# A graph attention layer's main loop: one-hot columns made a step ahead, two chunks of edges a PSUM bank, later copies and lasting count tiles

## The chip, the cores and the metric

The kernel runs on one core of one Trainium2 chip. The metric is the device time of one execution in microseconds (us); the times given are medians of several runs. The core has five engines with queues of their own: TensorE (PE; its weight loads appear as PEld), VectorE (DVE), ScalarE (ACT), GpSimd (POOL) and SyncE (SP), which here only issues transfers. Each queue is worked off in order.

## The reference

Two rounds of (graph layer, expert layer) over 3125 nodes with 256 features and 100000 edges sorted by destination. The change lies wholly in the first graph layer's first attention convolution:

```python
def gat_conv(x, src, dst, W, a_src, a_dst, bias, concat):
    N = x.shape[0]
    H, C = a_src.shape
    h = (x @ W).reshape(N, H, C)
    al_s = jnp.einsum('nhc,hc->nh', h, a_src)
    al_d = jnp.einsum('nhc,hc->nh', h, a_dst)
    e = jax.nn.leaky_relu(al_s[src] + al_d[dst], NEG_SLOPE)
    m = jax.ops.segment_max(e, dst, num_segments=N)
    ex = jnp.exp(e - m[dst])
    denom = jax.ops.segment_sum(ex, dst, num_segments=N)
    alpha = ex / denom[dst]
    out = jax.ops.segment_sum(h[src] * alpha[:, :, None], dst, num_segments=N)
    out = out.reshape(N, H * C) if concat else out.mean(axis=1)
    return out + bias
...
    loop = jnp.arange(N, dtype=edge_index.dtype)
    src = jnp.concatenate([edge_index[0], loop])
    dst = jnp.concatenate([edge_index[1], loop])
    h = gat_conv(x, src, dst, W1, att_src1, att_dst1, b1, concat=True)
    h = graph_norm(h, gn_w, gn_b, gn_ms)
    h = jax.nn.relu(h)
    out = gat_conv(h, src, dst, W2, att_src2, att_dst2, b2, concat=False)
```

There are four heads in the first convolution (W1 is 256 x 1024). Everything after it (graph norm, the second convolution, the expert layers, two graph convolutions) is untouched.

## The kernel before

Class `FirstLayer` does two jobs in one loop (`run`, from L2147 on), because both go through the edges in the same order of destinations.

**Counts.** The later layers want a matrix of edge counts, source by destination. The edges are taken in 391 chunks of 256 (`C1`, two columns of 128 each, `CT`). For a chunk, `make` builds two one-hot tiles for each column, `hot_key` (DVE, L1696) and `hot_lo` (DVE in L1699 for the first 20 chunks and every third one, else ACT in two steps, L1702 and, in `sharpen`, L1709). `multiply` (L1711, matmul in L1716) takes their product into a PSUM bank `ps` of three. `keep` (L1727) copies its columns but the first into the tile `acc` (ACT, L1733), and `add` (L1738) adds the first column (DVE, L1741), since neighbouring chunks share it. In pass i of the loop `count_step` (L1772) makes chunk i, multiplies i−1, keeps i−2 and adds i−3. The destinations are cut into ten pieces of 320 (`GS`, `GC`); at a piece's first chunk (`CUT`) `piece` (L1677) takes an `acc` tile of a pool of two, clears a part of it (L1686) and copies the 100 columns that the last piece has run over into it (L1688); `add_own` and `store_counts` then finish the last piece and write it to DRAM. `low_degrees` sums the first piece over PE (L1766).

**Edge sums.** For destinations from 256 on (`DN`), 283 chunks (`NE`), the layer is done sparsely. `fetch` (L1832) has POOL gather the 256 source rows of a chunk from a table in DRAM, two indirect transfers of 128 rows (L1834), into a ring `edge_rows` of 12 chunks (`RB`·`BC`); the place of a chunk is free when the chunk 12 earlier has been multiplied. Four chunks are a batch. One batch ahead of their use, `pick_terms` (PE, L1872, into a bank `aux` of two), `sum_terms` (DVE, L1881, which reads the bank and the gathered rows of the whole batch), `pick_slope` (L1888), `weigh_edges` (ACT, L1893) and `spread_edges` (DVE, L1899) make the weights. `multiply_edges` (L1903, eight matmuls in L1913) sums a chunk into one of four half banks `ps_edge`, and `add_edges` (L1918, DVE, L1926) adds this to `agg1`, a tile of 384 destinations (`GA`), one chunk later. `edge_step` (L1929) orders these. A finished tile of `agg1` goes through W1: `through_w1` (L2002) loads the inverse sums, scales on DVE (L2034) and has eight products (PE, L2042, into an `aux` bank); `put_first` (L2050) copies each from PSUM (ACT, L2053), stores it (L2054) and leaves its `bn_stats` (DVE, L2056) to the next pass. These are tasks in a queue, one a pass.

**Dense part.** The 256 first destinations are done with the counts of piece 0: `slope` and `exponent` on ACT, `weigh` on DVE, `multiply_dense` on PE (L2102), then `dense_end` and `dense_first`, which use `aux` banks too.

The order on PE, DVE and ACT within the loop is the order of the code (`in_order`, L108). The queues of SP and POOL are ordered by the scheduling of the whole program. So POOL also holds, from 693 us on, loads of x for a later stage between the gathers (L989). Where instructions use a position known only at run time, `where` (L1527) loads eight positions into registers at a time (`RG`). Passes before the loop (from L2194) do the first chunks; the loop runs until both jobs and all tasks are through. `d0` is the pass at which the dense part may begin, `share` the number of edge steps due.

Of the kernel before, what the change touches and what calls it, by code (L numbers as in the profile page):

```python
# [24 lines left out]
P = 128  # L25
# [23 lines left out]
RG = 8  # L49
# [1344 lines left out]
class FirstLayer:  # L1394
# [261 lines left out]
    def open_counts(self, ctx, pool):  # L1656
# [14 lines left out]
        self.acc_pool = ctx.enter_context(tc.tile_pool(name="acc", bufs=2, reuse_waits="tile"))  # L1671
        self.hot = ctx.enter_context(tc.tile_pool(name="hot", bufs=3, reuse_waits="tile"))
# [4 lines left out]
    def piece(self, g):  # L1677

        nc = self.nc
        acc = self.acc[g] = self.acc_pool.tile([P, NB, GC + EXT], F16, name="acc")
        if g == 0:
            nc.vector.memset(acc, 0.0)
        else:
            nc.vector.memset(acc[:, :, EXT if g in (1, GS - 1) else GC:], 0.0)  # L1686
        if g:
            nc.vector.tensor_copy(acc[:, :, :EXT], self.acc[g - 1][:, :, GC:])  # L1688
# [73 lines left out]
    def low_degrees(self):  # L1762
        nc = self.nc
        pd = self.aux.tile([P, 512], F32, name="aux")[:, :DN]
        for j in range(NB):
            nc.tensor.matmul(pd, lhsT=self.ones, rhs=self.acc[0][:, j, :DN], start=(j == 0),  # L1766
                             stop=(j == NB - 1))
        sums = self.work.tile([1, DN], F32, name="deg_low")
        nc.scalar.copy(sums, pd[0:1, :])
        nc.sync.dma_start(self.deg_row.rearrange("b p -> (b p)")[None, :DN], sums)  # L1770

    def count_step(self, i, beside=(lambda: None,) * 2):  # L1772
# [3 lines left out]
        if 1 <= i <= C1:  # L1776
            self.multiply(i - 1)
        if 3 <= i <= C1 + 2:
            self.add(i - 3)
        if 2 <= i <= C1 + 1:  # L1780
            self.keep(i - 2)
# [3 lines left out]
        if i == C1 + 2:  # L1785
            self.tasks.append(lambda: self.add_own(GS - 1))
            self.tasks.append(lambda: self.store_counts(GS - 1))
# [3 lines left out]
    def open_sums(self, ctx, w1, stats):  # L1791
# [11 lines left out]
        self.ps_edge = [banks[i % 2][:, i // 2 * 256:(i // 2 + 1) * 256] for i in range(4)]  # L1803
# [23 lines left out]
        self.ready, self.scaled, self.later = 0, 0, []  # L1827
# [101 lines left out]
    def edge_step(self, c):  # L1929
# [18 lines left out]
        if 0 < c <= NE:  # L1948
            self.add_edges(c - 1)
# [52 lines left out]
    def through_w1(self, q):  # L2002
# [34 lines left out]
        def product(h, f):  # L2037
            bank = (self.ps_counts.tile([P, 512], F32, name="ps") if self.counted else
                    self.aux.tile([P, 512], F32, name="aux"))
# [9 lines left out]

    def put_first(self, h, f, n0, n, ph, piece, true):  # L2050
        nc = self.nc
        out = self.work.tile([P, GA], F32, name="first", bufs=3)[:, :n]
        nc.scalar.copy(out, ph)  # L2053
        nc.sync.dma_start(self.first[h, :, f, n0:n0 + n], out)  # L2054

        self.later.append(lambda: nc.vector.bn_stats(self.stats[:, h, f, piece, :],  # L2056
                                                     out[:, :true]))
# [7 lines left out]
    def lead(self, s):  # L2065
# [5 lines left out]
        if j == 0:  # L2071
            pt = self.aux.tile([P, 512], F32, name="aux")
# [39 lines left out]
    def dense_end(self, i, po, turned):  # L2112
        nc = self.nc
        inv = self.work.tile([P, 1], F32, name="inv", bufs=4)
# [5 lines left out]
        def turn():  # L2120
            pt = self.aux.tile([P, 512], F32, name="aux")
# [6 lines left out]
    def dense_first(self, h, f, turned):  # L2128
        ph = self.aux.tile([P, 512], F32, name="aux")[:, :DN]
# [17 lines left out]
    def run(self, src_cols, dst_cols, dst_rows, x_in, keep, stats, u2):  # L2147

        tc, nc, k, I = self.tc, self.nc, self.k, self.I
        with ExitStack() as ctx:  # L2150
# [82 lines left out]
            i0, d0 = i, CUT[1] + 6  # L2233
# [5 lines left out]
            while i < C1 + 3 or e <= NE or s < last_s or self.tasks or self.later:  # L2239
# [9 lines left out]
                if i < C1 + 3:  # L2249
# [4 lines left out]
                self.counted = i >= C1 + 3  # L2254
                if i == d0:
                    self.lead(0)
                later, self.later = self.later, []
                if self.tasks:
                    self.tasks.popleft()()
                share = (FIRST * (i - i0) / (d1 - i0) if i < d1 else  # L2260
                         FIRST + (NE + 1 - FIRST) * (i - d1) / (C1 - d1))
                while e <= NE and e <= share:
                    self.edge_step(e)
                    if e == NE:
# [6 lines left out]
                if due:  # L2271
                    self.dense_step(s)
                    s += 1
                for f in later:
# [536 lines left out]
```

## Time and profile before

| | us |
|---|---|
| median of 7 runs (lowest to highest) | 2381.84 (2375.16 to 2385.69) |
| the profiled execution, its own time | 2379.65 |
| span of its profile | 2377.9 |
| before the first gather of rows | 0 to 84.9 |
| the loop, to the last W1 product | 84.9 to 899.8 |
| the later layers | to 2377.9 |
| busy over the span: PE, DVE, ACT, POOL | 2058.2, 1328.8, 1088.4, 808.9 |

Over the 820 us from 85 to 905, PE was busy 659.2 us, DVE 621.4, ACT 500.6 and POOL 603.3. The groups that the loop spends most on, with their busy time and mean length: gathers on POOL, L1834, 566 of 1.04 us (588.5); edge matmuls, L1913, 2264 of 0.29 us (331.0); one-hot columns on DVE, L1696, 782 of 0.33 us (234.8); count matmuls, L1716, 782 of 0.34 us (193.1); copies of counts on ACT, L1733, 391 of 0.46 us (178.3). A busy share says how long an engine worked, not whether anything else waited for it; for that the waits and the timeline are read.

In a row of a timeline the first number is the start, the second the length, both in us; what stands in brackets is how long the engine was idle before, and the instruction that ended this. A row of a wait lists the engine and line that waited, what it waited for, the total, the number of times and the longest.

### The profile page before, as it was taken

The numbers are of one execution on the slowest core, as the hardware profiler recorded it, in microseconds if no ns is written. First come the engines' busy times: TensorE is split into PE (matmuls) and PEld (weight loads), VectorE is DVE, ScalarE is ACT, GpSimd is POOL, SyncE is SP. The second block draws the span as 40 slices with busy tenths as digits, with TensorE's granted clock in tenths as the row PEclk, the third lists the DMA queues.
The fourth block names the chain that finished last, engine by engine and source line by source line (L and its number), as shares of the span: only waits on it lengthen the run. The fifth ranks groups of instructions, "written<-read, shape, count | busy, mean of one in ns | idle before, by whom it ended". The sixth has DMA issues, their size and how long they took to land. (4 is left out here: it accounts for less than half of the span.)

```text
span 2377.9 us, 35928 instructions
## 1 busy us (share of the span) xinstructions
PE 2058.2 (87%) x10508; PEld 1714.5 (72%) x10508; DVE 1328.8 (56%) x4374; ACT 1088.4 (46%) x2506; POOL 808.9 (34%) x802
## 2 busy tenths in 40 slices
PE   5377887878888878899998799979988979999996
PEld 5255766666676656788887688858877767888885
DVE  6988676777888672178888243333326664221221
ACT  4297656556666446044444244434434433222221
POOL 1477777777777732000001300000001213222221
PEclk9999999999999889999999799989999988999998
DMA  8445475756767759962221100033334435667772
GB/s 263 114 122 157 131 211 141 208 166 187 203 183 227 202 163 344 316 218 70 70 70 46 36 1 1 1 124 111 111 112 155 149 134 181 188 195 229 206 224 59
DMA packets 236987, 358.49 MB, mean 151 GB/s; under 512 B 37357, under 2 KB 178052, under 8 KB 233068
## 3 DMA queue, kind: packets, MB, share of 16 engines
q1 hardware_dynamic: 193611, 256.27, 33.5%
q0 software_dynamic: 39600, 95.33, 15.8%
q10 hardware_dynamic: 3568, 4.47, 0.7%
q8 instruction: 88, 1.44, 0.3%
q14 instruction: 120, 0.98, 0.1%
HBM read 270.26 MB, written 86.20 MB: 150 GB/s over the span
## 5 line engine op out<-in xcount | busy, mean ns | idle before, releaser
L1834 POOL DMA_INDIRECT edge_rows<-table,pick x566 | 588.5, 1040 | 177.8 <-issue 84.6
L1913 PE MATMUL edge_sums<-edge_moves,edge_rows 128*128 128x120 f32 x2264 | 331.0, 293 | 76.9 <-DVE agg L1926 74.0
L1913 PEld LDWEIGHTS edge_sums<-edge_moves,edge_rows 128*128 128x128 f32 x2264 | 308.3, 206 | 114.0 <-DVE agg L1926 90.6
L1092 PE MATMUL po<-parts,cnt_r 128*128 128x512 f32 x1250 | 318.5, 410 | 17.7 <-ACT cnt_r L1086 9.5
L1092 PEld LDWEIGHTS po<-parts,cnt_r 128*128 128x128 f32 x1250 | 240.1, 195 | 71.6 <-ACT cnt_r L1086 10.3
L854 PE MATMUL po<-h,w 128*128 128x257 f32 x1250 | 278.9, 384 | 7.2 <-DVE w L845 4.9
L854 PEld LDWEIGHTS po<-h,w 128*128 128x128 f32 x1250 | 237.4, 191 | 44.3 <-DVE w L845 6.9
L1716 PE MATMUL ps<-hot_key,hot_lo 128*128 128x350 f16 (+2 forms) x782 | 193.1, 336 | 83.9 <-DVE acc L1741 38.4
L1733 ACT CAST acc<-ps 128x325 f32 (+2 forms) x391 | 178.3, 456 | 143.5 <-PE ps L1716 107.5
L1696 DVE TENSOR_SCALAR hot_key<-iota_key,key 128x350 f16<-128x350 f16 (+2 forms) x782 | 234.8, 329 | 3.4 <-PE ps L1716 1.9
L2679 ACT ACTIVATE hid<-ph,ffn_b 128x256 f32<-128x256 f32 (+1 forms) x232 | 105.6, 455 | 264.3 <-PE ph L2677 261.8
L2677 PE MATMUL ph<-xe,ffn_w 128*128 128x256 f32 (+1 forms) x928 | 194.8, 368 | 3.8 <-DVE rt_xt L1023 3.8
L2692 POOL DMA_INDIRECT out<-y,to x53 | 82.6, 1558 | 316.8 <-DVE y L2691 172.6
L2687 PE MATMUL py<-ffn_w,hid 128*128 128x256 f32 x848 | 189.8, 381 | 0.4 <-ACT hid L2679 0.4
L2677 PEld LDWEIGHTS ph<-xe,ffn_w 128*128 128x128 f32 x928 | 165.3, 194 | 27.2 <-DVE rt_xt L1023 4.2
L2687 PEld LDWEIGHTS py<-ffn_w,hid 128*128 128x128 f32 x848 | 159.3, 191 | 21.1 <-ACT hid L2679 0.8
L839 ACT ACTIVATE z<-z,att_cols 128x640 f32<-128x640 f32 x125 | 103.1, 828 | 154.1 <-DVE z L837 131.3
L1702 ACT ACTIVATE hot_lo<-iota_key,lo 128x128 f16<-128x128 f16 x494 | 169.6, 394 | 0.0
L1716 PEld LDWEIGHTS <-hot_lo 128*128 128x128 f16 x782 | 73.2, 104 | 129.0 <-ACT hot_lo L1709 41.2
L1086 ACT CAST cnt_r<-cnt_h 128x1920 fp32r<-128x1920 f16 x50 | 89.8, 1799 | 117.1 <-PE po L1092 106.6
L2353 POOL IOTA earlier<- 128x128 f32 x1 | 0.2, 243 | 399.9 <-PE po L1092 399.9
L845 DVE TENSOR_TENSOR w<-z,cnt 128x640 f32<-128x640 f32 x125 | 106.7, 854 | 38.6 <-PE po L854 35.6
(419 smaller groups left out, 3245.4 us busy)
## 6 DMA issues: line engine op xcount, KB each, us to landing
ffn_w<-in_L_ffn_W SPq DMA_DIRECT2D x58, 1024.0 KB
cnt_h<-cnt SPq DMA_DIRECT2D x50, 800.0 KB
rows<-blank SPq DMA_DIRECT2D x109, 258.0 KB
cnt<-acc SPq DMA_DIRECT2D x50, 400.0 KB
cnt<-cnt SPq DMA_DIRECT2D x25, 800.0 KB
normed<-first_out SPq DMA_DIRECT2D x20, 640.0 KB
first_out<-first SPq DMA_DIRECT2D x56, 192.0 KB
edge_rows<-table,pick POOLq DMA_INDIRECT x566
```

Source lines behind the costliest of these rows:

```text
L845: nc.vector.tensor_tensor(w, zs.pop(t), cnts[u, g, j // 5][:, j % 5, :], ALU.mult)
L854: nc.tensor.matmul(pos[i][:, :D + 1], lhsT=w[:, ts(i, P)], rhs=moving[:, j, :D + 1], start=(j == 0), stop=(j == NB - 1))
L1092: nc.tensor.matmul(pos[b], lhsT=c[:, j - j0, ts(b, P)], rhs=parts[i][:, j].rearrange("p a m -> p (a m)"), start=(j == 0), stop=(j == NB - 1))
L1696: nc.vector.tensor_scalar(h[:, u, :NB * w], self.wide[:, :NB * w], self.key[:, t:t + 1], None, op0=ALU.is_equal)
L1702: nc.scalar.activation(l[:, u, :], self.wide[:, :P], AF.Abs, bias=self.lo[:, t:t + 1], scale=-1.0)
L1716: self.nc.tensor.matmul(ps[:, :n], lhsT=l[:, u, :], rhs=h[:, u, :n], start=(u == 0), stop=(u == CT - 1))
L1733: ins = self.nc.scalar.copy(self.acc[g][:, :, ds(o + 1, width(c) - 1)], self.parts[c][:, :, 1:])
L1834: self.nc.gpsimd.indirect_dma_start(out=self.ring[:, e % (RB * BT), :], out_offset=None, in_=self.table, in_offset=bass.IndirectOffsetOnAx ...
L1913: nc.tensor.matmul(ps[:, f * 4 * w:f * 4 * w + EW], lhsT=self.rows_of(m)[:, e, ts(f, P)], rhs=self.spread[m % 3][:, e * 5 * w:e * 5 * w + EW],
L2677: nc.tensor.matmul(ph, lhsT=w1[:, c, ts(f, P)], rhs=xe[:, c, :], start=(c == 0), stop=(c == 1))
L2679: nc.scalar.activation(hid[:, f, :], ph, AF.Gelu, bias=b1[:, f:f + 1])
L2687: nc.tensor.matmul(py, lhsT=hid[:, f, ts(i, P)], rhs=w2[:, f, :], start=(f == 0), stop=(f == NF - 1))
```

## The change

It alters the order of the loop and what lies in which bank; what is computed stays.

- `RG` goes from 8 to 16: positions are loaded sixteen at a time.
- `acc` is no longer a pool of two tiles taken anew for each piece, but two lasting tiles used in turn. The part beyond column 100 is cleared for pieces 1 and 9 alone; for pieces 2 to 8 the clearing of the last 100 columns is left out.
- The one-hot tiles have four buffers instead of three, and `count_step` multiplies chunk i−2, adds i−4 and keeps i−3. The loop is a pass longer, and `d0` a pass later.
- `ps_edge` holds chunks 0 and 1 of four in one bank and 2 and 3 in the other, where it held 0 and 2, and 1 and 3. `add_edges` comes two chunks after the product.
- `put_first` only notes its copy; the copy and the store are issued at the end of the next pass, and `bn_stats` a pass after that. A new `bank` hands out the `aux` banks: it keeps the copy that is still owed for the bank given out two requests earlier, and issues it first. `pick_terms` goes on taking its `aux` bank without it.
- `inv` has two buffers instead of four.

```diff
-RG = 8
+RG = 16
...
-        self.acc_pool = ctx.enter_context(tc.tile_pool(name="acc", bufs=2, reuse_waits="tile"))
-        self.hot = ctx.enter_context(tc.tile_pool(name="hot", bufs=3, reuse_waits="tile"))
+        room = ctx.enter_context(tc.tile_pool(name="acc", bufs=1, reuse_waits="tile"))
+        self.both = [room.tile([P, NB, GC + EXT], F16, name=f"acc{i}") for i in range(2)]
+        self.hot = ctx.enter_context(tc.tile_pool(name="hot", bufs=4, reuse_waits="tile"))
...
-        acc = self.acc[g] = self.acc_pool.tile([P, NB, GC + EXT], F16, name="acc")
+        acc = self.acc[g] = self.both[g % 2]
         if g == 0:
             nc.vector.memset(acc, 0.0)
-        else:
-            nc.vector.memset(acc[:, :, EXT if g in (1, GS - 1) else GC:], 0.0)
+        elif g in (1, GS - 1):
+            nc.vector.memset(acc[:, :, EXT:], 0.0)
         if g:
             nc.vector.tensor_copy(acc[:, :, :EXT], self.acc[g - 1][:, :, GC:])
...
-        if 1 <= i <= C1:
-            self.multiply(i - 1)
+        if 2 <= i <= C1 + 1:
+            self.multiply(i - 2)
+        if 4 <= i <= C1 + 3:
+            self.add(i - 4)
         if 3 <= i <= C1 + 2:
-            self.add(i - 3)
-        if 2 <= i <= C1 + 1:
-            self.keep(i - 2)
+            self.keep(i - 3)
...
-        self.ps_edge = [banks[i % 2][:, i // 2 * 256:(i // 2 + 1) * 256] for i in range(4)]
+        self.ps_edge = [banks[i // 2][:, i % 2 * 256:(i % 2 + 1) * 256] for i in range(4)]
...
-        if 0 < c <= NE:
-            self.add_edges(c - 1)
+        if 2 <= c <= NE + 1:
+            self.add_edges(c - 2)
...
+    def bank(self):
+
+        first = self.held.popleft()
+        self.held.append(None)
+        if first in self.copies:
+            self.copies.remove(first)
+            first()
+        return self.aux.tile([P, 512], F32, name="aux")
+
     def put_first(self, h, f, n0, n, ph, piece, true):
         nc = self.nc
         out = self.work.tile([P, GA], F32, name="first", bufs=3)[:, :n]
-        nc.scalar.copy(out, ph)
-        nc.sync.dma_start(self.first[h, :, f, n0:n0 + n], out)
-
-        self.later.append(lambda: nc.vector.bn_stats(self.stats[:, h, f, piece, :],
-                                                     out[:, :true]))
+
+        def copy():
+            nc.scalar.copy(out, ph)
+            nc.sync.dma_start(self.first[h, :, f, n0:n0 + n], out)
+            self.later.append(lambda: nc.vector.bn_stats(self.stats[:, h, f, piece, :],
+                                                         out[:, :true]))
+        if not self.counted:
+            self.held[-1] = copy
+        self.copies.append(copy)
...
-            i0, d0 = i, CUT[1] + 6
+            i0, d0 = i, CUT[1] + 7
...
-            while i < C1 + 3 or e <= NE or s < last_s or self.tasks or self.later:
+            while i < C1 + 4 or e <= NE + 1 or s < last_s or self.tasks or self.later or \
+                    self.copies:
...
                 later, self.later = self.later, []
+                copies = list(self.copies)
                 if self.tasks:
                     self.tasks.popleft()()
                 share = (FIRST * (i - i0) / (d1 - i0) if i < d1 else
-                         FIRST + (NE + 1 - FIRST) * (i - d1) / (C1 - d1))
-                while e <= NE and e <= share:
+                         FIRST + (NE + 2 - FIRST) * (i - d1) / (C1 - d1))
+                while e <= NE + 1 and e <= share:
...
+                for f in copies:
+                    if f in self.copies:
+                        self.copies.remove(f)
+                        f()
                 for f in later:
                     f()
```

In `low_degrees`, `lead`, `dense_end`, `dense_first` and the products of `through_w1`, `self.aux.tile(...)` becomes `self.bank()`.

More of the change, by code (lines that the diff above doesn't have):

```diff
@@ L1763, in low_degrees @@
         nc = self.nc
-        pd = self.aux.tile([P, 512], F32, name="aux")[:, :DN]
+        pd = self.bank()[:, :DN]
         for j in range(NB):
@@ L1784, in count_step @@
         beside[1]()
-        if i == C1 + 2:
+        if i == C1 + 3:
             self.tasks.append(lambda: self.add_own(GS - 1))
@@ L1826, in open_sums @@
         self.agg = {}
-        self.ready, self.scaled, self.later = 0, 0, []
+        self.ready, self.scaled, self.later, self.copies = 0, 0, [], []
+        self.held = deque([None, None])
     def rows_of(self, m):
@@ L2038, in product @@
             bank = (self.ps_counts.tile([P, 512], F32, name="ps") if self.counted else
-                    self.aux.tile([P, 512], F32, name="aux"))
+                    self.bank())
             ph = bank[:, :n]
@@ L2071, in lead @@
         if j == 0:
-            pt = self.aux.tile([P, 512], F32, name="aux")
+            pt = self.bank()
             for i in range(DB):
@@ L2113, in dense_end @@
         nc = self.nc
-        inv = self.work.tile([P, 1], F32, name="inv", bufs=4)
+        inv = self.work.tile([P, 1], F32, name="inv", bufs=2)
         nc.vector.tensor_scalar(inv, po[:, ONE:], 1e-30, None, op0=ALU.max)
@@ L2120, in turn @@
         def turn():
-            pt = self.aux.tile([P, 512], F32, name="aux")
+            pt = self.bank()
             for c in range(2):
@@ L2128, in dense_first @@
     def dense_first(self, h, f, turned):
-        ph = self.aux.tile([P, 512], F32, name="aux")[:, :DN]
+        ph = self.bank()[:, :DN]
         for c in range(2):
@@ L2248, in run @@
                           lambda b=beside[1]: [self.exponent(x) for x in b])
-                if i < C1 + 3:
+                if i < C1 + 4:
                     self.count_step(i, beside)
@@ L2253, in run @@
                     beside[1]()
-                self.counted = i >= C1 + 3
+                self.counted = i >= C1 + 4
                 if i == d0:
@@ L2260, in run @@
                 share = (FIRST * (i - i0) / (d1 - i0) if i < d1 else
-                         FIRST + (NE + 1 - FIRST) * (i - d1) / (C1 - d1))
-                while e <= NE and e <= share:
+                         FIRST + (NE + 2 - FIRST) * (i - d1) / (C1 - d1))
+                while e <= NE + 1 and e <= share:
                     self.edge_step(e)
-                    if e == NE:
+                    if e == NE + 1:
                         while self.scaled < AS - 1:
```

## The prediction

> **What bounds the kernel now.** The change touches one stretch, the first layer's loop, so I first looked for the engine that never rests in it. The windows view over that loop (columns: window, length, then busy time and instructions of PE, PEld, DVE, ACT and POOL, granted clock, DMA share, GB/s):
>
> ```profile
> 110.00:300.00 190.00, 145.45 (x1033) 119.36 (x1033) 150.06 (x735) 145.97 (x496) 145.51 (x147) 0.92 0.51 137
> 300.00:600.00 300.00, 250.40 (x1544) 203.38 (x1543) 216.36 (x812) 174.96 (x509) 231.89 (x224) 0.94 0.65 183
> 600.00:850.00 250.00, 215.16 (x1259) 170.48 (x1257) 197.62 (x667) 151.40 (x413) 197.07 (x196) 0.94 0.70 200
> ```
>
> PE is busy 83% of the middle window, DVE 72%, ACT 58%, POOL 77%: read as shares, PE looks like the limit. The timeline of POOL says otherwise. It runs the row gathers of L1834 and nothing else, and the next one always starts 0.30 us after the last:
>
> ```profile
> 424.28 0.95 POOL L1834 DMA_INDIRECT edge_rows<-table,pick  x1 [0.30 <-PE ps L1716]
> 425.53 0.95 POOL L1834 DMA_INDIRECT edge_rows<-table,pick  x1 [0.30 <-issue]
> ...
> 432.05 2.56 POOL L1834 DMA_INDIRECT edge_rows<-table,pick  x1 [0.30 <-issue]
> 434.91 0.95 POOL L1834 DMA_INDIRECT edge_rows<-table,pick  x1 [0.30 <-issue]
> ```
>
> The reader should see that the names behind "<-" change while the 0.30 does not: it is the price of going from one gather to the next, not a wait. The waits view of POOL between 110 and 850 has 0.3 as its longest entry in every row, so no gather waited for its ring place. I also paired each gather's start with the end of the eighth L1913 matmul of the chunk twelve earlier, which frees its place: the place was free 10.1 us earlier in the median, and never less than 0.4 us earlier (near 224 us, and 0.6 near 570). So one stream sets the loop, from 84.92 us to 859.4: 566 gathers of 0.945 us (534.9), 565 gaps of 0.305 (172.3), 53.6 us by which single gathers are longer, and 13.8 us for 23 of the x loads of L989 that sit between them (0.6 each): 774.6, against 774.5 measured.
>
> The other engines follow it. In the waits view over 200 to 950 us:
>
> ```profile
> PEld edge_sums L1913 <- DVE agg L1926: 90.6, 38, 6.0
> PE edge_sums L1913 <- DVE agg L1926: 74.0, 34, 5.6
> DVE edge_p L1881 <- DMA edge_rows<-table,pick: 68.6, 22, 5.2
> ACT first L2053 <- PE aux L2042: 62.8, 36, 4.3
> ACT acc L1733 <- PE ps L1716: 56.8, 65, 4.7
> PEld L1716 <- ACT hot_lo L1709: 25.1, 20, 5.3
> ```
>
> DVE stands at L1881 until a batch's last gather has landed; L1926 is behind it in DVE's queue, and PE waits for L1926. Most batches pass L1881 2 to 4 us after their last gather ends; where they fall 8 to 11 us behind (near 232, 358, 594, 681 and 842 us) they are back within a few batches, and no gather was held up by it.
>
> **What lengthens a gather.** DVE does. The 3.39 us memset and 0.77 us copy that begin the last piece of counts, beside POOL:
>
> ```profile
> 848.83 3.39 DVE L1686 MEMSET acc<- 128x4000 uint32 x1 [0.76 <-DMA x_rows<-in_x]
> 852.14 0.77 DVE L1688 COPY acc<-acc 128x2500 f16<-128x2500 f16 x1
> ```
> ```profile
> 847.44 1.04 POOL L1834 DMA_INDIRECT edge_rows<-table,pick  x1 [0.30 <-issue]
> 848.78 4.88 POOL L1834 DMA_INDIRECT edge_rows<-table,pick  x1 [0.31 <-issue]
> ```
>
> The gather begins with the memset and ends 0.76 us after the copy. All nine such pairs of the loop show the same 0.76 to 0.79. The seven small ones (memset 1.10, copy 0.77) stretched their gathers to 2.37, 2.56, 1.66, 2.37, 2.31, 2.68 and 2.30 us: 16.25, less 7 x 0.945, is 9.6 us lost.
>
> **The change, part by part.**
> *Lasting tiles of counts.* For pieces 2 to 8 the memset is not issued: 7 x 1.10 us of DVE go, the copy stays. Pieces 1 and 9 keep theirs (3.39 us each). What the seven copies alone will cost a gather no row shows. Bounds: nothing each, so 9.6 saved; or the whole 0.77 each time, 5.4, so 4.2 saved. A gather is held if the copy covers one point of its 1.25 us cycle, chance 0.77/1.25 = 0.62, then for half the copy: 0.24 each; with the 0.25 us add ahead of it counted in, 0.42. I take 0.33: 2.3 in all, 7.3 saved, because all nine holds end with the copy.
> One row speaks against it: the f32 memset of L1962 at 584.83 (0.81 us) left the gather beside it at 0.95. The uint32 memset above did not: its gather would have ended 2.4 us before the copy began. So the copy may hold POOL from ahead of its own start, and without the memset from one instruction earlier, which is in the 0.42.
> The Trainium skill, "SBUF — State Buffer", section "Who interferes with whom", says that a DVE instruction with at most one SBUF input, outside the two-port modes, does not contend with GpSimd, while a copy can enter such a mode. By that rule the memsets cost POOL nothing and the sum would be +1.6 instead of −5.7; the gather of 4.88 us disagrees, the L1962 row agrees.
> *One-hot columns a step ahead, four buffers.* L1696, L1699, L1702 and L1709 run as often as before; L1716 comes one pass later. This removes PE's waits for hot_lo (65.3 us for L1709 in the rows of L1716) and, with the later add, for L1741 (55.7). Cost nothing, gain nothing: they lie under the gather stream. If that cover were gone they would be worth up to those sums.
> *Two chunks a bank, sums a step later.* Same 283 adds (L1926, 0.22 to 0.35 us). The 164.6 us that PE and its weight loads wait for them are mostly DVE standing at L1881, which stays. On the path: 0.
> *W1's copies a step later.* Same 72 copies of 0.36 to 0.48 us (L2053) and same stores on SP; ACT no longer stands 62.8 us for L2042. Each store waits on SP for its later copy, ahead of the window loads (L1847); those are fetched two batches, some 20 us, ahead. 0, unless PE runs short of a bank (the slower rival).
> *Sixteen registers a load.* 85 loads of 0.6 us on DVE's queue and 49 of 0.55 on ACT's become half as many. Between nothing saved (twice as long) and 25 us of DVE's queue; either way under the 71.0 us that DVE waits for gathers. 0.
> *The end.* The last chunk's sums are added two passes after its product instead of one, and counts run one pass more. The last passes each take 1.30 us (L1716 at 866.82, 868.12, 869.43): +1.3, and one more L1741 (0.25) behind the scaling of L2034: together +1.6. Bounds 0 and 3.2 (two passes and more). After that the order of W1's last products, 877.66 to 899.8, is the same, waiting for by_node's load.
> *The start.* The first gather waits for L1591 to end at 84.06; nothing ahead of it moves but one add. 0 (−0.1 to +0.3).
>
> Sum: −7.3 + 1.6 = **−5.7 us**. The profiled execution took 2379.65 us (span 2377.9 and 1.75 around it), so 2374.0; the median of the seven runs, 2381.84, lies 2.2 above that, which gives 2376.1. I say 2376.
>
> **Rivals.**
> *Slower: a bank short in W1's products.* The terms' product (L1872) still takes one of the same two banks and stands outside the new queue of held ones. In a stretch of eight products it falls twice; then PE may stand until the late copy, or until L1881 has read the terms, and all of PE's queue (counts, dense steps, the edge products that free the ring) stands with it. DVE's wait there is 71.0/25 = 2.8 us. Seven stretches x 2 x 2.8 = 40 us of PE, of which the 10 us of lead swallows most; where the lead had already sunk under 5 us (three times in the loop) nothing does: 3 x 2 x 2.8 = 17. With the −5.7, +11: 2393. It decides once a stretch loses more lead than it has. Against it: PE idles 14 to 17% and the change frees PE elsewhere.
> *No saving from the memsets* (something queued behind them holds POOL): +1.6, 2383.
> *The loop bound by its engines after all.* Then removing L1709's waits and the like could bring some 30 us (half of 65.3): 2352. Against it: not one POOL wait over 0.3 us.
> *The x loads fall elsewhere.* Their place in POOL's queue is not written in the code; it comes from the scheduling of the whole program. All 23 behind the gathers: −13.8 more, 2362; one waiting for its dense step: a few us more.
>
> **How the numbers follow.** Forecast 56%, its own range 2369 to 2382 (4.2 to 9.6 saved, 0 to 3.2 lost, the other DVE holds, 53.6 − 9.6 = 44 us, falling some 4 us better or worse, and 2 for a median). Bank rival 22%, no saving 10%, engines 5%, x loads 7%. About 0.2% (4.8 us) is what a measurement of this kernel tells from no change. Of the forecast 44 lie beyond it, with engines 5 and x loads 5: faster 0.54. Same: 12 of the forecast, 9 of no saving, 1 of the bank rival: 0.22. Slower: 21 of the bank rival, 1 and 2 of the rest: 0.24. Leaving out the far half of the bank rival and the engines' case gives 2367 to 2391.
>
> **What would show it.** Right: gathers still 1.25 us apart with 0.30 idle, the last one starting near 851 instead of 858.3, gathers beside L1688 under 1.75 us in pieces 2 to 8, PE's and ACT's named waits smaller and no shorter loop for it, L1881 still waiting for gathers. Wrong: idle over 0.3 us ahead of gathers, PE waiting ahead of L1872 or L2042 (bank rival); gathers beside L1688 still over 2 us (no saving); the loop shorter by more than its gathers' sum (engines).

## The result, and the profile after

The changed kernel takes 2385.31 us in the median of 26 runs (2379.32 to 2394.66), the kernel before 2378.57 in the median of 63. The ratio is 1.0031, with a 95% interval of 1.0023 to 1.0039: slower by about 7 us, where 5.7 us faster were forecast. A second set of 12 runs (e9) gave 1.0024 (1.0013 to 1.0034).

The first profile after took 2377.15 us, less than any of the 26 runs, and ends 2.5 us ahead of the profile before; by itself it would show a gain. The 1.46 ms behind the loop differ by up to 11 us between executions (1457 to 1468 us in two profiles of each kernel). So I look at the loop alone, which ends with the first Relu of the next stage, and at two profiles of each kernel (the second ones are runs e9 and e10 below). All marks in us:

| | before | changed | difference of means |
|---|---|---|---|
| first gather starts | 84.9, 84.9 | 86.1, 85.9 | +1.1 |
| gathers, first start to last end | 774.5, 779.2 | 766.1, 770.3 | −8.6 |
| last gather's end to last batch's sums (L1881, now L1883) | 3.1, 3.3 | 10.4, 8.9 | +6.5 |
| these to the last add of edges (L1926, now L1928) | 9.0, 10.1 | 14.0, 14.0 | +4.5 |
| last add to last copy of W1's products | 28.8, 28.4 | 31.3, 31.0 | +2.6 |
| last copy to the first Relu | 9.3, 9.2 | 10.3, 10.4 | +1.1 |
| end of the loop | 909.5, 914.9 | 918.3, 920.5 | +7.2 |

The 7.2 us are close to the 6.7 between the medians; since the two profiles before differ by 5.4 us among themselves, so close an agreement is partly luck. The gathers did become shorter, and everything behind them became longer by more. From here on the lines are those of the changed kernel, one or two behind the old numbers.

First the windows view of the changed kernel over the loop, in the same columns as before:

```profile
110.00:300.00 190.00, 146.26 (x1027) 123.71 (x1026) 148.47 (x732) 146.74 (x498) 144.38 (x147) 0.91 0.51 137
300.00:600.00 300.00, 249.30 (x1552) 202.84 (x1553) 215.57 (x815) 177.83 (x511) 231.11 (x227) 0.95 0.65 184
600.00:850.00 250.00, 216.01 (x1249) 169.90 (x1249) 192.36 (x661) 152.56 (x412) 196.35 (x200) 0.93 0.70 201
```

POOL (the fifth pair) issues 200 instructions in the last window where it issued 196, and DVE's busy time falls from 197.6 to 192.4: four more instructions through by 850 us, and the missing memsets. The waits view, 200 to 950 us:

```profile
ACT acc L1734 <- PE ps L1717: 124.9, 108, 8.7
DVE edge_p L1883 <- DMA edge_rows<-table,pick: 85.0, 30, 5.2
...
PEld edge_sums L1915 <- DVE agg L1928: 67.8, 27, 5.1
...
PE edge_sums L1915 <- DVE agg L1928: 56.6, 25, 4.7
...
PEld aux L1874 <- DVE edge_turn L1861: 21.8, 14, 6.2
...
ACT first L2066 <- PE aux L2044: 12.2, 26, 1.0
```

Waits that the change aims at became smaller: ACT's at W1's copies from 62.8 to 12.2 us, PE's for the sums from 74.0 to 56.6. Others grew instead: DVE's for gathers from 68.6 to 85.0, and ACT's for the products of counts, first row, from 56.8 to 124.9. The body of the loop runs at POOL's pace, as the prediction said, but not quite without a stop: behind the clearing of piece 1, between 235 and 247 us, gathers waited for a place in the ring, 1.1 us beyond the usual 0.30 in this profile and 5.0 in the second. Neither profile before has such a wait, and what brought it was not tested.

The gathers beside the counts' copies behave as predicted too. The timeline of DVE, then of POOL, where piece 3 begins (the gather there took 2.56 us before):

```profile
433.33 0.84 DVE L1689 COPY acc<-acc 128x2500 f16<-128x2500 f16 x1
```
```profile
432.54 0.94 POOL L1836 DMA_INDIRECT edge_rows<-table,pick  x1 [0.30 <-PE edge_sums L1915]
433.79 1.15 POOL L1836 DMA_INDIRECT edge_rows<-table,pick  x1 [0.30 <-PE edge_sums L1915]
```

Over pieces 2 to 8 the lengthening falls from 9.6 us to 1.6 (8.7 to 1.7 in the second profiles).

Then the end. POOL's last two gathers, and DVE's timeline between the sums of batch 69 and those of batch 70, the last:

```profile
849.98 0.98 POOL L1836 DMA_INDIRECT edge_rows<-table,pick  x1 [0.30 <-issue]
851.26 0.94 POOL L1836 DMA_INDIRECT edge_rows<-table,pick  x1 [0.30 <-issue]
```
```profile
847.61 0.19 DVE L1883 TENSOR_TENSOR edge_p<-aux,edge_rows 128x32 f32<-128x32 f32 x1 [0.42 <-issue]
...
855.31 3.39 DVE L1687 MEMSET acc<- 128x4000 uint32 x1 [0.76 <-issue]
858.63 0.77 DVE L1689 COPY acc<-acc 128x2500 f16<-128x2500 f16 x1
...
860.61 0.34 DVE L1861 TENSOR_SCALAR edge_turn<-edge_turn,part_place 96x256 f32<-96x256 f32 x1
...
862.62 0.17 DVE L1883 TENSOR_TENSOR edge_p<-aux,edge_rows 128x24 f32<-128x24 f32 x1
```

The gathers are over at 852.2, and the last batch's sums still come at 862.62. Before, they came at 862.47, and DVE had been idle for only 0.40 us (2.39 in the second profile):

```profile
862.47 0.18 DVE L1881 TENSOR_TENSOR edge_p<-aux,edge_rows 128x24 f32<-128x24 f32 x1 [0.40 <-DMA x_rows<-in_x]
```

Sooner last gathers alone could not have brought these sums forward by much more than that. In the changed kernel the clearing of piece 9, which stood ahead of batch 69's sums (848.83), now stands behind them. There it holds no gather any more but everything behind it on DVE, and through that PE:

```profile
861.00 1.03 PE L1874 MATMUL aux<-window,edge_turn 96*128 96x12 f32 x4 [5.72 <-DVE edge_turn L1861]
...
885.47 0.99 PE L1717 MATMUL ps<-hot_key,hot_lo 128*128 128x500 f16 x2 [8.33 <-DVE acc L1742]
886.26 3.99 PE L2044 MATMUL ps<-agg,w_all 128*128 128x384 f32 x7
```

The second and third row are the end of the tail: a product of counts waits 8.33 us for a bank whose add stands behind the scaling on DVE, and the next products of W1 start at 886.26, where they started at 877.66. The scaling itself waits for the load of by_node, before and after:

```profile
873.93 3.50 DVE L2034 TENSOR_TENSOR agg<-agg,by_node 128x1024 f32<-128x1024 f32 x3 [2.52 <-DMA by_node<-inverse]
```
```profile
881.75 3.50 DVE L2036 TENSOR_TENSOR agg<-agg,by_node 128x1024 f32<-128x1024 f32 x3 [5.15 <-DMA by_node<-inverse]
```

(1.90 and 4.71 in the second profiles.) Between the last batch's sums and the last add of edges PE is what is busy. The windows view of that stretch, before and after:

```profile
862.47:871.41 8.94, 8.94 (x66) 7.67 (x65) 8.04 (x36) 7.42 (x21) 0.00 (x0) 1.00 0.11 34
```
```profile
862.62:876.60 13.98, 13.04 (x84) 10.85 (x83) 10.88 (x44) 9.45 (x26) 0.00 (x0) 0.90 0.07 20
```

PE had 84 matmuls to do there instead of 66 (84 and 51 in the second profiles): with counts and sums later, more of the loop's last work lies behind the last batch's sums.

### The profile page after: what moved, and what is told of

It is laid out like the page before. It is cut to its first block, busy times and chain, and to the rows that moved or that the text cites. A ratio compares the mean times of both kernels' runs of the same rounds, so it can differ in the third digit from the quotient of the medians.

```text
span 2375.4 us, 35673 instructions
## 1 busy us (share of the span) xinstructions
PE 2050.6 (86%) x10508; PEld 1712.0 (72%) x10508; DVE 1321.2 (56%) x4367; ACT 1092.6 (46%) x2506; POOL 799.7 (34%) x802
## 5 line engine op out<-in xcount | busy, mean ns | idle before, releaser
L1836 POOL DMA_INDIRECT edge_rows<-table,pick x566 | 579.2, 1023 | 180.0 <-issue 80.5
L1915 PE MATMUL edge_sums<-edge_moves,edge_rows 128*128 128x120 f32 x2264 | 328.7, 292 | 62.5 <-DVE agg L1928 56.6
L1092 PEld LDWEIGHTS po<-parts,cnt_r 128*128 128x128 f32 x1250 | 238.5, 194 | 67.6 <-ACT cnt_r L1086 10.4
```

What stands on the lines that cost most here:

```text
L1092: nc.tensor.matmul(pos[b], lhsT=c[:, j - j0, ts(b, P)], rhs=parts[i][:, j].rearrange("p a m -> p (a m)"), start=(j == 0), stop=(j == NB - 1))
L1836: self.nc.gpsimd.indirect_dma_start(out=self.ring[:, e % (RB * BT), :], out_offset=None, in_=self.table, in_offset=bass.IndirectOffsetOnAx ...
L1915: nc.tensor.matmul(ps[:, f * 4 * w:f * 4 * w + EW], lhsT=self.rows_of(m)[:, e, ts(f, P)], rhs=self.spread[m % 3][:, e * 5 * w:e * 5 * w + EW],
```

## The experiments

Each ratio is against the kernel before on the same chip. Theory A at the outset: the loss lies behind the last gather, because counts and sums run a pass later.

**e1, the lasting tiles alone** (in the kernel before).

```diff
-        self.acc_pool = ctx.enter_context(tc.tile_pool(name="acc", bufs=2, ...))
+        room = ctx.enter_context(tc.tile_pool(name="acc", bufs=1, ...))
+        self.both = [room.tile([P, NB, GC + EXT], F16, name=f"acc{i}") for i in range(2)]
-        else:
-            nc.vector.memset(acc[:, :, EXT if g in (1, GS - 1) else GC:], 0.0)
+        elif g in (1, GS - 1):
+            nc.vector.memset(acc[:, :, EXT:], 0.0)
```

> The kernel before with one part of the change alone: the two lasting tiles of counts, so the memsets of pieces 2 to 8 are gone. The mark used in all of these is the end of the loop: the first Relu of the next stage, at 909.5 us in the profile before and 918.3 in the one after. Theory A (POOL's gathers set the loop up to some 50 us before its end, and the change loses its gain behind the last gather, because the counts and the sums run a pass later): the last gather ends 6 to 9 us sooner (near 852), and with counts and sums where they were most of that arrives: end of the loop at 902 to 907, median 2 to 7 us under before. Theory B (the last 50 us are set by DVE and PE from far ahead, whatever POOL does): the last gather ends as much sooner, but the end of the loop stays within 1.5 us of 909.5 and the median within 2 us of before.

Ratio 0.9996 (0.998 to 1.0013). The gathers took 774.9 us, no less than before; the loop ended at 911.9. Neither theory had this. The twelve runs lie 1.2 us under before, and at most 4.8 by the interval, where theory A had 2 to 7. Gathers beside the counts' memsets and copies were lengthened by 8.8 us instead of 17.5, but those beside DVE's other instructions by 45.1 instead of 36.2.

**e2, the one-hot columns back** (in the changed kernel).

```diff
-        if 2 <= i <= C1 + 1:
-            self.multiply(i - 2)
-        if 4 <= i <= C1 + 3:
-            self.add(i - 4)
+        if 1 <= i <= C1:
+            self.multiply(i - 1)
+        if 3 <= i <= C1 + 2:
+            self.add(i - 3)
...
-            self.keep(i - 3)
+            self.keep(i - 2)
```

> The changed kernel with the one-hot columns no longer a step ahead: product one pass after the columns, copy two, add three, three buffers, and the loop one pass of counts shorter. Theory A: the later counts are the larger part of the loss, since they move the clearing of piece 9 (3.39 + 0.77 us) from ahead of batch 69's sums to between 69's and 70's, and put one more pass of counts behind the last edges. End of the loop 5 to 8 us sooner than 918.3 (910 to 913), median 4 to 8 us under the changed kernel. Theory C (the late copies of W1's products and their bank cost the time): within 1.5 us of 918.3. Theory D (sixteen registers a load cost it, 1.28 us each on DVE's queue): within 1.5 us of 918.3 too.

Ratio 1.0006 (0.9989 to 1.0022), 4 to 6 us under the changed kernel, as theory A has it. Its reason is not shown: piece 9's clearing still fell between batch 69's sums (853.03) and batch 70's, at 855.03. The loop ended at 915.7, later than expected; from the last batch's sums to the end it took 51.0 us, against 55.6.

**e3, the sums of edges back.**

```diff
-        if 2 <= c <= NE + 1:
-            self.add_edges(c - 2)
+        if 0 < c <= NE:
+            self.add_edges(c - 1)
...
-        self.ps_edge = [banks[i // 2][:, i % 2 * 256:(i % 2 + 1) * 256] for i in range(4)]
+        self.ps_edge = [banks[i % 2][:, i // 2 * 256:(i // 2 + 1) * 256] for i in range(4)]
```

> The changed kernel with the sums of edges added one pass after their product again, the chunks of a bank as before (0 and 2, 1 and 3) and the loop one pass of edges shorter. Theory A: this is the smaller part of the loss: end of the loop 1.3 to 4 us sooner than 918.3, median 1 to 4 us under the changed kernel; PE's waits for the sums grow back from 67.8 and 56.6 us to some 80 without a later end of the gathers. Theory C and theory D: within 1 us of 918.3. Should the layout of the banks be what matters, the waits for the sums return and the last gather ends later.

Ratio 0.9998 (0.9984 to 1.0013): more than the 1 to 4 us expected. From the last batch's sums to the loop's end 53.6 us, the loop's end 915.0.

**e4, W1's copies at once again.**

```diff
...
-        if not self.counted:
-            self.held[-1] = copy
-        self.copies.append(copy)
+        copy()
```

> The changed kernel with W1's products copied at once again, without the queue of held banks. Theory A: the copies lie beside other work; ACT's wait for PE ahead of them grows back from 12.2 to some 60 us, and the end of the loop stays within 1.5 us of 918.3, the median within 2 us of the changed kernel. Theory C: end of the loop 5 us sooner or more, median 4 us or more under the changed kernel. In the last stretch of products (before 877.7 to 899.8, after 886.3 to 907.6) either shows in the spacing of the copies.

Ratio 1.0028 (1.0011 to 1.0045), loop's end 919.8: as slow as the changed kernel. Theory C falls.

**e5, the edges spread over two more passes of counts.**

```diff
-                         FIRST + (NE + 2 - FIRST) * (i - d1) / (C1 - d1))
+                         FIRST + (NE + 2 - FIRST) * (i - d1) / (C1 + 2 - d1))
```

> The changed kernel with the edges spread over two more passes of counts (C1 + 2 in place of C1 in their share), so that at a given edge the counts stand where they stood before the change. In the changed kernel the sums of the last batch (L1883) fall ahead of eleven adds of counts, before it they fell ahead of nine, and each pass there takes 1.5 to 1.7 us. Theory A (the loss is counts left over behind the last gathers): last add of edges 2 to 4 us sooner after the last batch's sums than the 14.0 us of the changed kernel, end of the loop 3 to 6 us sooner than 918.3, median 3 to 6 us under the changed kernel. Rival (the later sums of edges themselves: their product, bank and add): the last add as late, end of the loop within 1.5 us.

Ratio 1.0041 (1.0025 to 1.0057), loop's end 920.7. From the last batch's sums to the end it took only 50.6 us, but those sums came at 870.1 instead of 862.6. So theory A was wrong in one point: it is not that counts are left over. The same work in other order ends no sooner.

**e6, piece 9's memset cut to 80 columns.**

```diff
-        elif g in (1, GS - 1):
+        elif g == 1:
             nc.vector.memset(acc[:, :, EXT:], 0.0)
+        elif g == GS - 1:
+            nc.vector.memset(acc[:, :, N - g * GC - 5:GC], 0.0)
```

> The changed kernel with piece 9's memset cut to the 80 columns behind the last edge's (some 0.85 us in place of 3.39). It stands at 855.3 us, 3 us behind the last gather, with PE waiting 5.7 us and ACT 5.4 for what is queued behind it on DVE. Theory A: 1.5 to 2.5 us of it arrive: end of the loop at 916 to 917, median 1 to 3 us under the changed kernel. Rival (DVE has that time to spare there, since PE sets the last passes): within 0.7 us of 918.3.

Ratio 1.0006 (0.9993 to 1.0019), 4 to 6 us under the changed kernel, more than expected. The profiled execution was the slowest of its 11 (2387.65 us; the loop's end 922.3), so its end says little; the step that the edit touches is in it: from batch 69's sums to batch 70's 11.9 us, against 15.0 and 13.5.

**e7, both** of the last two edits.

> Both at once: the edges spread over two more passes of counts, and piece 9's short memset. Theory A: the two gains add, since one shortens what stands ahead of the last batch's sums and the other what stands behind them: last gather near 852, end of the loop at 908 to 913, median 5 to 9 us under the changed kernel, that is at the time of before or up to 3 us under it. If the end of the loop is set by PE alone: as with the spreading alone, within 1 us.

Ratio 1.0013 (1.0002 to 1.0025), loop's end 919.4. The spreading is a loss, so there are not two gains to add; its loss and e6's gain add up within the intervals.

**e8, eight registers a load** (`RG = 8`).

> The changed kernel with eight registers a load. In the changed kernel DVE stands 2.06 us at its load of sixteen ahead of the first add of counts (74.3 us), where the kernel before had a load of eight 0.6 us long there and its first one beside another wait. Theory A: the first gather starts 0.8 to 1.4 us sooner than 86.09, and the end of the loop follows by as much; median 0.5 to 2 us under the changed kernel. Theory D (the longer loads cost it in the loop and its end too): end of the loop 3 us sooner or more.

Ratio 0.9997 (0.9983 to 1.001), 6 to 8 us under the changed kernel. That is theory D's gain, but its profile, of one of the slower executions, does not show it: the first gather came 0.5 us sooner (85.6), the stretch behind the last batch's sums took 55.4 us as in the changed kernel, and the loop ended at 920.1. The cause stays open.

**e9 and e10, both kernels again, unaltered.**

> The changed kernel once more, unaltered, for a second profile and for times on the same chip as the kernels beside it. Its first profile, 2377.15 us, was faster than all of its other 26 runs. If the first profile's loop is typical: end of the loop within 3 us of 918.3, and the rest of the program longer than the 1457.1 us it took there (1460 to 1468 as in the other profiles). If the loop's end is a matter of chance from execution to execution: 5 us or more away from 918.3. Median 5 to 10 us over before.

> The kernel before once more, unaltered, for a second profile. If its first profile's loop is typical: end of the loop within 3 us of 909.5, last gather within 3 us of 859.4, and gathers lengthened by DVE by 50 to 57 us in all (53.8). If what DVE takes from the gathers is a matter of chance in the phases of both: outside of that.

They are the second columns of the table. The changed kernel's loop is steady. That of before ended 5.4 us later than in its first profile: gathers beside DVE's instructions other than the counts' lost 42.8 us instead of 36.2. This is chance from execution to execution, and it is nearly as large as the gain that e1 was to show; e1's profile can't settle that term.

**e11, columns and sums both back** (e2 and e3 together).

> The changed kernel with both the one-hot columns and the sums of edges back where they were; what is left of the change is the lasting tiles, the late copies and the sixteen registers. Each undone alone brought the median back to that of before (ratios 1.0006 and 0.9998). Theory A (the two delays share one loss, the work behind the last batch's sums): no more than either alone, median within 3 us of before, end of the loop 908 to 913, from last batch's sums to last add 9 to 10 us. If the two losses are separate and add: median 5 us or more under before.

Ratio 0.9984 (0.997 to 0.9997), 8.7 us under the changed kernel on the same chip (2373.92 to 2382.60). From the last batch's sums to the end 47.7 us, as before the change (47.0, 47.6). The two delays together cost 9 us; what is left of the change is a small gain. In its profile the gathers took 776.3 us, as long as before, although the memsets of pieces 2 to 8 are gone: piece 9's clearing stands ahead of batch 69 again and holds a gather.

**e12, no long memset in the loop** (in the kernel before, with the lasting tiles).

```diff
+                nc.gpsimd.memset(self.both[1], 0.0)
...
-        elif g in (1, GS - 1):
-            nc.vector.memset(acc[:, :, EXT:], 0.0)
+        elif g == GS - 1:
+            nc.vector.memset(acc[:, :, N - g * GC - 5:GC], 0.0)
```

> The kernel before with lasting tiles and no long memset in the loop at all: POOL clears the second tile while it idles (between 30 and 69 us), and piece 9 clears 80 columns only. This takes 2 x 3.4 us of DVE and two gathers of 4.9 us out of the loop, beside the seven small memsets. Theory A' (removed holds of gathers are handed back, since gathers then meet DVE's other long instructions more often, as with the lasting tiles alone: 8.7 us fewer beside the counts' copies, 8.9 more beside the rest): lengthening still 45 to 54 us, median within 2.5 us of before. Theory POOL (each hold removed shortens the loop): lengthening 33 to 40 us, last gather 12 to 18 us sooner than 859.4, median 6 us or more under before.

Ratio 0.9985 (0.9971 to 0.9999). The gathers took 767.7 us with 46.6 us of lengthening, within theory A'; the median, 3.8 us under before, lies between the two. But POOL did the new memset, written ahead of the loop, earlier than meant, and held DVE there. DVE's first casts, which take 0.16 and 0.68 us in the profile before, and POOL's row:

```profile
6.42 6.07 DVE L1668 CAST ident_h<-ident 128x128 f16<-128x128 f32 x1
6.50 6.52 DVE L1427 CAST rows_f<-rows 98x1024 f32<-98x1024 int32 x1
```
```profile
3.52 8.88 POOL L2190 MEMSET acc<- 128x10500 f16 x1
```

The first gather came at 90.1 us for it: 5.2 of the gain given back at the start.

**e13, one gather in eight left out; e14, the last 22 left out** (both in the changed kernel, in `fetch`).

```diff
+            if c >= RB * BC and e % BT == BT - 1:
+                continue
```
```diff
+        if c >= BC * (NBAT - 3):
+            return
```

> The changed kernel with one gather in eight left out from the fourth batch on (67 of 566; those edges then use rows of earlier edges, so the output is another). POOL has 84 us less to do, nothing else changes. If POOL's stream sets the loop (the prediction's claim): the last batch's sums and the end of the loop come 50 to 85 us sooner than 863 and 919. If PE, DVE and ACT set it, pass by pass, with POOL only close behind them: 0 to 20 us sooner, and gathers then stand idle for free places in the ring, more than 40 us in all.

> The changed kernel without the gathers of its last three batches (22 of 566, 27 us of POOL; those edges use older rows). Theory A (in the last 50 us POOL no longer sets anything, so what was won ahead of them is lost there): the last batch's sums stay at 861 to 866 and the end of the loop at 916 to 921. If POOL's stream still sets the end: both come 5 us sooner or more.

e13: 84 us less for POOL brought the last batch's sums 49 us sooner (814.5) and the loop's end 50 (869.4). POOL sets the body; some 50 us further down the other engines do. The waits view (110 to 800 us) shows the change of roles: POOL waits for places in the ring, 6.1 us at the longest and some 34 us in all beyond the usual 0.30 of each, and DVE's wait for gathers, 82.1 us in the changed kernel over the same stretch, is down to 20.1:

```profile
POOL edge_rows L1838 <- PE edge_sums L1917: 70.5, 121, 6.1
...
DVE edge_p L1885 <- DMA edge_rows<-table,pick: 20.1, 11, 3.7
```

e14 (one execution, like e13): with the last gather over at 820.2 us, 32 to 36 us sooner, the last batch's sums came at 860.8 and the loop's end at 916.2, 3 us under the mean of the two profiles. DVE's timeline there:

```profile
846.85 0.19 DVE L1885 TENSOR_TENSOR edge_p<-aux,edge_rows 128x32 f32<-128x32 f32 x1
853.45 3.39 DVE L1687 MEMSET acc<- 128x4000 uint32 x1 [0.76 <-issue]
856.76 0.77 DVE L1689 COPY acc<-acc 128x2500 f16<-128x2500 f16 x1
...
860.75 0.17 DVE L1885 TENSOR_TENSOR edge_p<-aux,edge_rows 128x24 f32<-128x24 f32 x1
```

The 13.9 us from one batch to the next are there with no gather in sight. Batches 68 to 70, whose gathers are left out, have their sums at 837.6, 846.8 and 860.8; in the first profile of the changed kernel they had them at 837.8, 847.6 and 862.6. From the sums of batch 67 on (822.1 and 822.3), 96 us before the loop's end, POOL sets next to nothing.

**e15 and e16, the version that follows**: lasting tiles, columns, sums and registers as before the change, and both long memsets cut; e15 with the late copies, e16 without.

```diff
+        elif g == 1:
+            nc.vector.memset(acc[:, :, GC:], 0.0)
+        elif g == GS - 1:
+            nc.vector.memset(acc[:, :, N - g * GC - 5:GC], 0.0)
```

> What the runs so far leave over: lasting tiles and W1's late copies, with one-hot columns, sums and registers as before, and both long memsets cut (piece 1 clears the 100 columns behind its own, 1.1 us; piece 9 the last 80, 0.85). The nearest run (lasting tiles, late copies, sixteen registers) had 0.9984 of before. Expected: 2 to 5 us of DVE and of gathers less, end of the loop 904 to 909, median 4 to 8 us under before. Theory A' (every hold that goes is handed back to others): as the nearest run, 2 to 4 us under.

> The same without the late copies: the kernel before with lasting tiles and both long memsets cut. It tells whether the late copies are worth anything by themselves. Theory A: they are not, since ACT's waits for PE lie beside other work: end of the loop and median within 2 us of the run beside it. If they are: 3 us or more behind it.

Ratios 0.9964 (0.995 to 0.9979) and 0.9971 (0.9957 to 0.9985): 2368.14 and 2370.48 us beside 2377.16. The loops of their profiles ended at 902.9 and 904.4. Both beat both kernels; the late copies by themselves can't be told from nothing. In e15 the gathers took 763.2 us and the last batch's sums followed 4.1 us behind them, with the 0.89 us memset again ahead of batch 69:

```profile
832.95 0.17 DVE L1885 TENSOR_TENSOR edge_p<-aux,edge_rows 128x32 f32<-128x32 f32 x1
...
838.87 0.89 DVE L1689 MEMSET acc<- 128x1000 uint32 x1
839.68 0.77 DVE L1691 COPY acc<-acc 128x2500 f16<-128x2500 f16 x1
840.97 0.19 DVE L1885 TENSOR_TENSOR edge_p<-aux,edge_rows 128x32 f32<-128x32 f32 x1 [0.15 <-DMA x_rows<-in_x]
...
852.26 0.18 DVE L1885 TENSOR_TENSOR edge_p<-aux,edge_rows 128x24 f32<-128x24 f32 x1
```

**e17, the sums one step later still** (the edit below); **e18, the columns a step ahead put into e15.**

```diff
-        if 2 <= c <= NE + 1:
-            self.add_edges(c - 2)
+        if 3 <= c <= NE + 2:
+            self.add_edges(c - 3)
```

> The changed kernel with the sums of edges one step later still (three passes after their product, the loop one more pass of edges). From the last batch's sums to the end of the loop the changed kernel takes 55.6 and 55.4 us in its two profiles, 51.0 with the columns back, 47.7 with columns and sums back: the sums' one step is 3.3 us there. Theory A (each step of delay costs its pass behind the last batch's sums): 58 to 60 us, median 2 to 5 us over the changed kernel. Rival (the first step cost by the layout of banks or a wait that a second one doesn't repeat): 55 to 56.5 us, median within 1.5 us of the changed kernel.

> The fastest kernel so far (lasting tiles, short clears, late copies; 0.9964 of before) with the one-hot columns a step ahead put in alone. Theory A: counts end one pass further behind the edges: from the last batch's sums to the end of the loop 4 to 6 us more than the 50.7 us there, median 2 to 6 us over that kernel (ratio 0.9973 to 0.9990). Rival (the step ahead costs only where piece 9's long memset then falls between the last batches, which is cut here): within 1.5 us of 50.7 us and of its median.

Ratios 1.0046 (1.0031 to 1.006) and 0.9946 (0.9929 to 0.9963), but on a chip on which the kernel before took 2513.41 us, 135 more than elsewhere. The loop is where that time went: in e18 its gathers took 894.7 us, with 122 stops of POOL of over 0.35 us among them (none in the profile before), while PE stood still with no releaser that the profile shows. PE's waits over 110 to 980 us (matmuls, then weight loads) and one of them in the timeline:

```profile
PE edge_sums L1917 <- issue: 59.6, 33, 12.7
```
```profile
PEld edge_sums L1917 <- issue: 76.2, 49, 12.8
```
```profile
118.16 2.03 PE L1917 MATMUL edge_sums<-edge_moves,edge_rows 128*128 128x120 f32 x8 [12.71 <-issue]
```

So POOL didn't set the body of the loop there, and the two runs don't decide what they were made for. From the last batch's sums to the end e17 took 56.1 us and e18 49.9, near the changed kernel's 55.5 and e15's 50.7: a hint that a delay is not a fixed price per step. On the other chips this stretch took 47.7 us with neither delay (e11), 51.0 with the later sums alone (e2), 53.6 with the columns alone (e3) and 55.5 with both; but e12 and e15, with neither, took 50.3 and 50.7, so not all of such a difference is the delays'. What each costs alone, and why, stays open; that they cost 9 us together is shown by e11's runs, and its profile puts it behind the gathers.

## Why the prediction was wrong

- **"One stream sets the loop."** Right for the body (e13). Wrong from the sums of batch 67 on, the last 96 us (e14), and this is the step that failed: the 7.3 us saved on the stream were added to the loop's end as if the last gather set it. The last gather ended 7.5 us sooner (means of two profiles each), batch 69's sums came 4.9 sooner and batch 70's 1.0. The rows had shown the place: I listed 842 us among the batches that fall 8 us behind, and ahead of the last batch's sums DVE stood idle for only 0.40 us.
- **The memsets, 7.3 us.** Right beside the copies: 9.6 us of lengthening became 1.6. On the stream it was less. Up to batch 67's last gather the stream is 3.5 us shorter (737.7 and 742.1 before, 734.3 and 738.5 after), with 3.1 us of new waits for the ring in that; the other 5.1 come in the last 22 gathers, among which no memset was removed, mostly because piece 9's clearing no longer holds one of them. So the last gather started near the 851 that I had named (851.26) in part by luck. Alone, the lasting tiles gave 1.2 us (e1).
- **Pieces 1 and 9 "keep theirs".** Wrong, though not one instruction of them changes. Piece 9's 4.2 us fell between the last two batches, from POOL's stream onto DVE's and PE's path: 9.3 and 11.5 us from batch 69's sums to 70's became 15.0 and 13.5, and 11.9 with the memset cut (e6). It is not the whole of it, since e2 has the memset there too and took 11.7.
- **"The end": 1.6 us (0 to 3.2).** Measured +8.2 from the last batch's sums, and gone with both delays undone (e11). I had priced one pass at 1.30 us and one add at 0.25. Behind those sums stand eleven adds of counts where there were nine, and eight of edges where there were seven, and the passes grew too: up to the last add the seven took 9.0 and 10.1 us, the eight 14.0 both times, of which PE was busy 13.0: +4.5. The scaling of W1's tile then waits 2.7 us longer for the load of by_node, which makes most of the next +2.6, and the next stage starts 1.1 later still.
- **What stays open.** Undoing either delay, cutting piece 9's memset (e6) or loading eight registers (e8) each took back 4 to 8 us by the medians, about the whole loss every time. The tails in the profiles of e6 and e8 are unchanged (55.6 and 55.4 us), so how these effects combine is not shown.
- **The start, 0.** +1.1 us. The timeline of DVE in the changed kernel shows a stop with no releaser:

```profile
74.85 0.24 DVE L1700 TENSOR_SCALAR hot_lo<-iota_key,lo 128x128 f16<-128x128 f16 x1
76.43 0.27 DVE L1697 TENSOR_SCALAR hot_key<-iota_key,key 128x200 f16<-128x200 f16 x1 [1.35 <-issue]
```

  It is a load of sixteen registers, 2.06 us long from 74.28. Ahead of the add that now comes a pass later it stands in the open; before, the first load of eight (0.86 us at 68.74) lay beside another wait. With the columns back the first gather starts at 84.6 (e2).
- **Sixteen registers a load** came out at the dear end of its bounds: 43 loads of 1.28 us on DVE (55.1) for 85 of 0.67 (57.3), and 25 of 1.35 on ACT (33.8) for 49 of 0.59 (28.9). Nothing is saved there, and e8 makes a price likely that I had put at 0.
- **One-hot columns, sums and copies at 0 in the body**: right in that the body stayed with POOL. Of the waits that I named, PE's for hot_lo shrank (L1709 65.3 us, L1710 now 11.2), the one for the add of counts did not (55.7, now 58.0), and ACT's for PE's counts grew. What I missed is that the price of a delay can be paid where the cover ends.
- **Rivals.** The bank rival's time (2393, +11) was nearer than the forecast's, but not its mechanism: PE's 15.6 us ahead of L1874, and its weight loads' 21.8, are waits for DVE's edge_turn, not for a bank, and with the copies at once the time stays (e4). Its first sign, idle over 0.3 us ahead of gathers, did appear (1.1 and 5.0 us), but e4 has it too (3.8).

## What to carry to other kernels

A stream that never idles sets the loop only as far as its last member's consumer follows at once: read the lag between the two batch by batch, and cost the stretch behind the point where it opens by the other engines. Delaying a step of a software pipeline can be free under cover and still cost where the cover ends (8.2 us here for two delays), together with whatever rare instruction (a clear, a hand-over) the delay moves there. One profile of a loop that varies by 5 us can't settle a term of 7; take two of each kernel, and compare stages, not ends.

## What the runs showed of the hardware

- The hold on a gather follows the memset's length: 4.88 us beside 3.39 + 0.77, 1.90 (839.35 in e15's timeline of POOL) beside 0.89 + 0.77, 1.15 beside the copy alone. The Trainium skill, "SBUF — State Buffer", section "Who interferes with whom", says that a DVE instruction with at most one SBUF input, outside the two-port modes, does not contend with GpSimd; by that, a memset outside those modes should not. But a copy stands behind each of them, and the f32 memset at 584.83, with no copy behind it, held nothing: whether the memset holds the gather or the copy that waits behind it, no run here tells.
- The other way round too: while POOL's memset of 8.88 us ran, a DVE cast of 0.68 us lasted 6.52 (e12).
- On DVE and ACT a load of registers costs nearly by the register: 0.67 us for eight and 1.28 for sixteen on DVE, 0.59 and 1.35 on ACT. On SP it is 1.05 and 1.52.
- The kernel before took 2378 us on most chips and 2513 on one; in e17's and e18's profiles from there, the later layers took as long as elsewhere (1464 and 1463 us), so the difference lies within the one loop.
